# The skip term D u in a scan's gate: a TensorE product with a diagonal, or one VectorE operation on the sum in PSUM

## The chip, the cores and the metric

The kernel runs on one core of a Trainium2 chip (trn2). The metric is the device time of one execution in microseconds. Three executions of the kernel before took 5039.27, 5041.66 and 5051.98 us; the median, 5041.66 us, is the time before.

## The reference, cut to what matters

The input x holds 8 images of 384 channels by 32 x 32 pixels, so 1024 tokens each. Layer 0 is a Mamba block (a selective scan with 16 states per channel) that runs over the tokens forward and, with the same weights, backward; a depthwise convolution stands beside it. Layer 1 is causal attention with 6 heads and, on the first five images, a feed-forward part with binarized weights. All in fp32.

```python
u = silu((uc + conv1d_b[None, :, None]).transpose(0, 2, 1))
...
h = dA * h + dBu
return (h, jnp.einsum('bdn,bn->bd', h, c))
...
y = ys.transpose(1, 0, 2) + u * D_param
y = y * silu(z)
return jnp.einsum('bld,od->blo', y, out_proj_w)
...
fwd = mamba(x_flat, *mparams)
bwd = jnp.flip(mamba(jnp.flip(x_flat, axis=1), *mparams), axis=1)
g = (fwd + bwd) * scale_mod
```

The line that the change concerns is `ys + u * D_param`: a skip term with one weight D per channel. As both directions share z and the output projection, the kernel adds the two directions before the gate: (y_fwd + y_bwd + D (u_fwd + u_bwd)) silu(z).

## The kernel before, in words

Channels lie on the 128 partitions, in 3 chunks (c), tokens on the free axis in 2 halves of 512 (h). `before_scan` makes, for each image, the normed input, the projections, the two convolved u, their sum "us", the gate z and the scan's inputs, and leaves them in DRAM. `attention` and `feed_forward` are layer 1. The scan is cut into 768 units of two states each, one channel chunk, one direction and one half. A unit goes through six steps:

- `s_load` and `s_row` (L112) bring the inputs; SP issues all these loads in one queue.
- `s_first` (L588): POOL multiplies to g, 128 x 1024. There are six buffers for g.
- `s_scan`: ACT makes the decay da in PSUM (L601), DVE scans it, twice 512 elements (L606), POOL weighs g with C's rows (L612).
- `s_sum` (L620): PE transposes g in eight 128 x 128 blocks and adds them up in the one PSUM bank "y". At the end of a run ACT copies y into a tile yt (L635) or DVE adds it to one (L639).
- `s_gate` (L641 to L671), at the last unit of each channel chunk and half, so 48 times: it loads us and z (tags with one buffer each), takes a bank with the tag "pt" (two banks, shared with attention's transposes and others), puts the skip term and the transposes back of the two yt into it, multiplies the gate z by it on DVE (L668), and stores the product (L670).

In the kernel before, the skip term is a product on PE (L654): us is the moving operand, 128 x 512, and the stationary one is diagd, three 128 x 128 matrices with D on their diagonal, built once by DVE at the start (L183). It opens the bank's accumulation, and the eight transposes (L659, two yt of four blocks) add to it.

The order of the work is a merged list. `slots` puts the steps of neighbouring units together, `spread_over` and the list `timed` weave them between the steps of layer 1 by costs that are written with each step. The Tile framework then schedules each engine's instructions by its own model, so that an edit in one step can move others: the final order in the engines' queues isn't the order of the text. [...]`pin` keeps some instructions in the order of the program.

Of the kernel before, what the change touches and what calls it, by code (L numbers as in the profile page):

```python
# [12 lines left out]
ALU = mybir.AluOpType  # L13
# [4 lines left out]
P = 128  # L18
B, C, H, W = 8, 384, 32, 32
L = H * W  # L20
NC = C // P
# [28 lines left out]
V_NORM, V_CW, V_CB, V_DTB, V_D, V_DW, V_DWB, V_BP, V_B2, V_ALOG = 0, 1, 5, 6, 7, 8, 17, 18, 19, 20  # L50
# [4 lines left out]
def kernel(  # L55
# [16 lines left out]
    nc = tc.nc  # L72
# [11 lines left out]
    def ctile(name, shape, dt=F32):  # L84
        return const.tile(shape, dt, name=name, tag=name)
# [13 lines left out]
    def bank(name, tag=None):  # L99
        if tag is None:  # L100
            turn[0] += 1
            tag = ("s", "pt")[turn[0] % 2]
        return ps.tile([P, HB], F32, name=name, tag=tag, bufs=BANKS[tag])

    def half(h):
        return slice(h * HB, (h + 1) * HB)

    def chunk(c):
        return slice(c * P, (c + 1) * P)

    def load(dst, src):
        nc.sync.dma_start(out=dst, in_=src)  # L112
# [17 lines left out]
    vec = ctile("vec", [P, NC, NV])  # L130
# [8 lines left out]
    for d in range(2):  # L139
        nc.scalar.dma_start(out=wdt[d * DW : d * DW + RANK, :], in_=w_dt)  # L140
        nc.scalar.dma_start(
            out=wdt[d * DW + RANK : d * DW + RANK + 1, :],
# [13 lines left out]
    ident = ctile("ident", [P, P])  # L156
# [21 lines left out]
    amat = ctile("amat", [P, NC, NS])  # L178
    nc.scalar.activation(amat, vec[:, :, V_ALOG : V_ALOG + NS], AF.Exp)
    nc.vector.tensor_scalar(amat, amat, -1.0, None, ALU.mult)  # L180
    diagd = ctile("diagd", [P, NC, P])
    for c in range(NC):
        nc.vector.tensor_scalar(diagd[:, c, :], ident, vec[:, c, V_D : V_D + 1], None, ALU.mult)  # L183
    rssm = ctile("rssm", [P, 1])
    nc.vector.tensor_tensor(rssm, sc[:, 0:1], sc[:, 1:2], ALU.mult)
    rsh = ctile("rsh", [P, 1])
# [454 lines left out]
    def s_gate(u):  # L641

        if not u.last:
            return
        b, c, h = u.b, u.c, u.h
        yts = sst.pop(("yt", b, c, h))
        both = []
        for what in ("us", "z"):
            t = sp.tile([P, HB], F32, name=f"{what}h_{u.name}", tag=what, bufs=1)
            load(t, spilled[b, what, c][:, half(h)])  # L650
            both.append(t)
        us, sz = both
        tp = bank(f"yb_{u.name}", "pt")
        nc.tensor.matmul(  # L654
            out=tp, lhsT=diagd[:, c, :], rhs=us, start=True, stop=False, skip_group_check=True
        )
        for yt in yts:
            for i in range(QT):
                nc.tensor.matmul(  # L659
                    out=tp[:, chunk(i)],  # L660
                    lhsT=yt[:, i, :],
                    rhs=ident,
                    is_transpose=True,
                    start=False,
                    stop=(yt is yts[-1] and i == QT - 1),
                    skip_group_check=True,
                )
        nc.vector.tensor_tensor(sz, sz, tp, ALU.mult)  # L668
        t = dram.tile([P, HB], F32, name=f"sgy_{u.name}", tag=f"sp_gy_{c}_{h}")
        nc.sync.dma_start(out=t, in_=sz)  # L670
        spilled[b, "gy", c, h] = t  # L671
# [421 lines left out]
    def slots(lo, hi):  # L1093
        def at(f, k):
            if 0 <= k < len(units):
                f(units[k])

        def slot(k):
            at(s_load, k + AHEAD + 2)
            at(lambda u: s_row(u, 0), k + AHEAD + 2)  # L1100
            at(lambda u: s_row(u, 1), k + 2)
            at(s_first, k + AHEAD)
            at(s_scan, k)
            at(s_sum, k - 1)
            at(s_gate, k - 1)

        return [(lambda k=k: slot(k), 5.0) for k in range(lo, hi)]
# [113 lines left out]
```

## Time and profile before

The profiled execution took 5052.48 us, its span from the first to the last instruction is 5050.7 us. The mean granted TensorE clock is 0.883 of full speed.

| what | value |
|---|---|
| median of the runs | 5041.66 us |
| profiled execution / its span | 5052.48 / 5050.7 us |
| busy PE, DVE, ACT, POOL | 4072.5, 3605.3, 2667.4, 3689.9 us |
| L654, product with the diagonal | x96 records, 57.3 us busy, mean 683 ns |
| L659, transposes back in the gate | x384, 63.5 us busy, mean 303 ns |
| L668, gate product on DVE | x48, 32.0 us busy, mean 667 ns |
| L635, ACT's copy of y to yt | x96, 55.7 us busy, mean 580 ns |
| DMA | 696.35 MB, mean 138 GB/s |

How it is read: a group's line gives the file's line, the engine, what is written from what, the count, the busy time and the mean of one, and then the idle time of the engine just before these instructions with what ended it (the releaser). An fp32 matmul shows as two records, so 48 products are 96 records. Matmuls overlap in the records: what one holds of PE's queue is better read from its start to the next one's start. A line of waits reads "who waited <- for whom: us in total, times, longest".

### The profile page before, as it was taken

To read this page: it belongs to the slowest core of one execution; us is meant where nothing else is said; L and a number is where in the kernel's file an instruction comes from. 1 tells how busy PE (TensorE), PEld (TensorE's weight loads), DVE (VectorE), ACT (ScalarE), POOL (GpSimd) and SP (SyncE) were. 2 spreads that over 40 slices of the span, in tenths; PEclk is the share of its full clock that TensorE was granted. 3 is DMA by queue.
4 is the path that set the end of the run, shared out by engine and by line. 5 is a ranking of instruction groups with operands and counts; after the bars stand their busy time and mean duration, and the time that the engine had idled before them with its cause. 6 is when DMAs were issued, how large, how long until landed. Compare 5 with 4: busy or idle time off the path is not lost. (4 is left out here: it accounts for less than half of the span.)

```text
span 5050.7 us, 50731 instructions
## 1 busy us (share of the span) xinstructions
PE 4072.5 (81%) x16458; PEld 2180.7 (43%) x16458; DVE 3605.3 (71%) x4775; ACT 2667.4 (53%) x4850; POOL 3689.9 (73%) x1944
## 2 busy tenths in 40 slices
PE   4687787888888888788788888887787978978899
PEld 1243343444444444344444444443454444444444
DVE  6887988676887767786778867688766666676623
ACT  4565664564554655545656446555465355464426
POOL 0578687896868976778876688867788988888700
PEclk7788797989889889888999889998898989989999
DMA  6554546323453334463334633334533334334210
GB/s 227 204 175 160 200 155 229 109 88 118 152 187 135 119 115 154 139 200 111 103 134 143 213 111 128 110 123 155 194 132 106 118 108 143 109 101 139 88 58 26
DMA packets 365009, 696.35 MB, mean 138 GB/s; under 512 B 30104, under 2 KB 88904, under 8 KB 364744
## 3 DMA queue, kind: packets, MB, share of 16 engines
q1 hardware_dynamic: 355232, 676.97, 40.0%
q10 hardware_dynamic: 9512, 16.15, 0.9%
q8 instruction: 130, 2.13, 0.2%
q14 instruction: 135, 1.11, 0.1%
HBM read 527.33 MB, written 165.68 MB: 137 GB/s over the span
## 5 line engine op out<-in xcount | busy, mean ns | idle before, releaser
L588 POOL TENSOR_TENSOR g<-ud,bc 128x1024 f32<-128x1024 f32 x768 | 1837.9, 2393 | 654.0 <-PE y L620 523.0
L612 POOL TENSOR_TENSOR g<-g,bc 128x1024 f32<-128x1024 f32 x768 | 1819.4, 2369 | 194.9 <-DVE g L606 132.4
L601 ACT ACTIVATE da<-dl,amat 128x512 f32<-128x512 f32 x1536 | 1055.9, 691 | 1515.1 <-DVE g L606 1489.8
L606 DVE TENSOR_TENSOR_SCAN g<-da,g 128x512 f32<-128x512 f32 x768 | 907.7, 1210 | 509.6 <-POOL g L588 496.3
L606 DVE TENSOR_TENSOR_SCAN g<-da,carry,g 128x512 f32<-128x512 f32 x768 | 955.1, 1271 | 403.9 <-POOL g L588 374.5
L620 PE MATMUL y<-ident,g 128*128 128x128 f32 x6144 | 920.6, 297 | 210.3 <-POOL g L612 122.3
L620 PEld LDWEIGHTS y<-ident,g 128*128 128x128 f32 x6144 | 766.9, 153 | 644.3 <-issue 345.5
L786 PE MATMUL s<-k,q 64*128 64x512 f32 (+3 forms) x1152 | 394.6, 602 | 134.6 <-DVE nm L800 113.5
L800 DVE CUSTOM_DVE_ANT_0 pr<-s,cmask 128x512 f32<-128x512 f32 (+3 forms) x576 | 298.9, 544 | 179.3 <-PE s L786 159.9
L810 ACT ACTIVATE pr<-pr,nm 128x512 f32<-128x512 f32 (+3 forms) x576 | 348.4, 606 | 125.1 <-DVE nm L800 123.5
L862 PE MATMUL pt<-ident,pr 128*128 128x128 f32 x1728 | 302.1, 304 | 83.5 <-ACT ptn L864 38.5
L992 PE MATMUL hp<-t,w 128*128 128x512 f32 x720 | 339.3, 618 | 25.4 <-DMA w<-w1s 21.2
L1036 PE MATMUL yp<-h,w 128*128 128x512 f32 x720 | 331.9, 620 | 32.0 <-DMA w<-w2s 27.6
L341 PE MATMUL in<-xn,win 128*128 128x512 f32 x576 | 291.2, 651 | 36.5 <-DVE xc L463 15.9
L862 PEld LDWEIGHTS pt<-ident,pr 128*128 128x128 f32 x1728 | 207.0, 152 | 243.5 <-ACT ptn L864 94.3
L875 PE MATMUL av<-ptn,v 128*64 128x512 f32 (+3 forms) x1152 | 274.3, 559 | 23.2 <-DVE o L889 17.2
L611 POOL COPY carry<-g 128x2 f32<-128x2 f32 x384 | 87.7, 228 | 271.2 <-DVE g L606 271.2
L864 ACT COPY ptn<-pt 128x512 f32<-128x512 f32 (+3 forms) x576 | 254.7, 473 | 55.5 <-PE pt L862 53.5
L725 PE MATMUL qp<-t,wqk 128*128 128x512 f32 x576 | 267.8, 616 | 14.7 <-DVE t L302 12.5
L400 DVE SCALAR_TENSOR_TENSOR loc<-xn,vec,loc 128x496 f32<-128x496 f32 (+3 forms) x384 | 259.5, 722 | 20.3 <-ACT loc L389 19.0
L786 PEld LDWEIGHTS s<-k,q 64*128 64x128 f32 x1152 | 134.8, 206 | 266.5 <-DVE nm L800 190.1
L1036 PEld LDWEIGHTS yp<-h,w 128*128 128x128 f32 x720 | 141.9, 201 | 204.7 <-issue 177.2
(153 smaller groups left out, 4753.4 us busy)
## 6 DMA issues: line engine op xcount, KB each, us to landing
bc<-rows SPq DMA_DIRECT2D x512, 512.0 KB, 4.1
dl<-sdl SPq DMA_DIRECT2D x160, 256.0 KB, 2.9
ud<-sud SPq DMA_DIRECT2D x160, 256.0 KB, 2.7
t<-st SPq DMA_DIRECT2D x63, 512.0 KB, 5.1
su<-u SPq DMA_DIRECT2D x48, 512.0 KB, 3.6
du<-su SPq DMA_DIRECT2D x96, 256.0 KB, 3.8
sdl<-du SPq DMA_DIRECT2D x96, 256.0 KB, 2.9
sud<-du SPq DMA_DIRECT2D x96, 256.0 KB, 2.7
```

The lines of the kernel that those rows point to most:

```text
L341: nc.tensor.matmul(out=mp, lhsT=st["win", c][:, k, i, :], rhs=st["xn"][:, k, half(h)], start=(k == 0), stop=(k == NC - 1),)
L588: pin(nc.gpsimd.tensor_tensor(g, ud, sst["bc", 0, u.b, u.part, u.n], ALU.mult))
L601: nc.scalar.activation(da, sst["dl", u.b, u.c, u.part], AF.Exp, scale=amat[:, u.c, n : n + 1])
L606: nc.vector.tensor_tensor_scan(gi[:, ::step], da[:, ::step], gi[:, ::step], first, ALU.mult, ALU.add)
L612: pin(nc.gpsimd.tensor_tensor(g, g, sst["bc", 1, u.b, u.part, u.n], ALU.mult))
L620: nc.tensor.matmul(out=y[:, j, :], lhsT=g[:, i, chunk(j)], rhs=ident, is_transpose=True, start=(u.opens and i == 0 and j == 0), stop=(u.cl ...
L786: mm = nc.tensor.matmul(out=ss[e][:, : k1 - k0], lhsT=st["q"][rows_of(e), c, chunk(qi)], rhs=st["k"][rows_of(e), c, k0:k1], start=True, st ...
L800: nc.vector.tensor_tensor_reduce(out=x, in0=ss[e][:, :w], in1=mask, scale=-1.0, scalar=-MASKED, op0=ALU.add, op1=ALU.min, accum_out=m,)
L810: nc.scalar.activation(x, x, AF.Exp, bias=m, scale=-1.0, accum_out=rs[:, i, e, kb : kb + 1])
L862: nc.tensor.transpose(pt[:, chunk(i)], pr[:, e, chunk(j % QT)], ident)
L992: nc.tensor.matmul(out=hp, lhsT=st["w1"][:, c, chunk(m % 2)], rhs=st["xn"][:, c, half(h)], start=(c == 0), stop=(c == NC - 1),)
L1036: nc.tensor.matmul(out=yp, lhsT=st["w2", k // 6][:, k % 6, :], rhs=st["h", k // NC][:, k % NC, half(h)], start=(k == 0), stop=(k == NF - 1),)
```

## The change

The diagonal matrices and the products with them are taken out. The first transpose of the gate now opens the bank's accumulation. Behind the transposes one DVE operation (scalar_tensor_tensor) computes us times D, D being a column with one value per partition, plus the sum in PSUM, and writes it back to the same bank; the gate product follows as before.

```diff
-    diagd = ctile("diagd", [P, NC, P])
-    for c in range(NC):
-        nc.vector.tensor_scalar(diagd[:, c, :], ident, vec[:, c, V_D : V_D + 1], None, ALU.mult)
...
         us, sz = both
         tp = bank(f"yb_{u.name}", "pt")
-        nc.tensor.matmul(
-            out=tp, lhsT=diagd[:, c, :], rhs=us, start=True, stop=False, skip_group_check=True
-        )
         for yt in yts:
             for i in range(QT):
                 nc.tensor.matmul(
...
                     is_transpose=True,
-                    start=False,
+                    start=(yt is yts[0] and i == 0),
                     stop=(yt is yts[-1] and i == QT - 1),
                     skip_group_check=True,
                 )
+        nc.vector.scalar_tensor_tensor(tp, us, vec[:, c, V_D : V_D + 1], tp, ALU.mult, ALU.add)
         nc.vector.tensor_tensor(sz, sz, tp, ALU.mult)
```

## The prediction

> **What bounds the kernel now.** I read the page's head first, then the table of who waits for whom on POOL and DVE, then every gate (the end of a scan, where the skip term enters) in the timeline, then the stretches around the gates.
>
> ```profile
> PE 4072.5 (81%) x16458; PEld 2180.7 (43%) x16458; DVE 3605.3 (71%) x4775; ACT 2667.4 (53%) x4850; POOL 3689.9 (73%) x1944
> ```
>
> No engine is full. PE is the busiest, and the scan runs in a ring: POOL makes g (L588), DVE scans it (L606), POOL weighs it (L612), PE adds it into y (L620), and that frees the buffer for POOL. Who is late in the ring is read from POOL's waits:
>
> ```profile
> POOL g L588 <- PE y L620: 523.0, 203, 16.0
> POOL carry L611 <- DVE g L606: 271.2, 28, 49.0
> POOL g L612 <- DVE g L606: 132.4, 18, 26.8
> ...
> POOL g L588 <- DVE g L606: 7.5, 4, 6.9
> ```
>
> POOL waits 523.0 us for PE and 271.2 + 132.4 + 7.5 = 411 us for DVE. So PE is the later partner in 523 / 934 = 0.56 of it, DVE in 0.44. These are my shares for how much of a change on either engine reaches the end. DVE in turn waits 870.8 us for POOL's L588: it often has time over.
>
> Now one gate of image 1, in the timeline of all engines (start, length, engine, line, operation, in brackets the idle time before it and its releaser):
>
> ```profile
> 1763.00 1.09 PE L620 MATMUL y<-ident,g 128*128 128x128 f32 x8
> ...
> 1763.93 1.02 PE L654 MATMUL yb<-ush,diagd 128*128 128x512 f32 x2
> ...
> 1764.79 0.60 PE L659 MATMUL yb<-ident,yt 128*128 128x128 f32 x4
> ...
> 1767.23 0.56 ACT L635 COPY yt<-y 128x512 f32<-128x512 f32 x1
> ...
> 1767.84 1.05 PE L659 MATMUL yb<-ident,yt 128*128 128x128 f32 x4 [2.45 <-ACT yt L635]
> 1767.91 2.34 DVE L606 TENSOR_TENSOR_SCAN g<-da,g 128x512 f32<-128x512 f32 x2 [1.61 <-POOL g L588]
> ...
> 1770.16 0.66 DVE L668 TENSOR_TENSOR zh<-zh,yb 128x512 f32<-128x512 f32 x1
> ...
> 1771.72 0.42 PEld L862 LDWEIGHTS pt<-ident,pr 128*128 128x128 f32 x4 [0.90 <-DVE zh L668]
> ```
>
> The diagonal product comes right behind the last y and holds PE's queue for 1764.79 - 1763.93 = 0.86 us. Then PE turns the first partial sum (four transposes) and stands for the second one, which ACT copies only at 1767.23. In 22 of the 48 gates PE stands there, 58.7 us in all. DVE's gate product comes late, behind two scans, and PE's next pt bank waits for it.
>
> **What the Trainium skill says.** "VectorE: DVE Perf Modes", section "Why PSUM operands drop a tier": an fp32 operation with an operand in PSUM runs at the plain rate of one element per cycle. Its errata section gives (N+151)/0.96 ns for an fp32 tensor_tensor, 691 ns at 512. The trace agrees roughly: L668 took 667 ns, and the form that the change adds is there as L369 (tile in SBUF, scalar column, sum read and written in PSUM): 746 ns. The same page, "The DRAIN you can't avoid", says that the next DVE operation doesn't start before the pipe is empty. Here it starts a little earlier: 0.58 to 0.60 us behind the start of L668, and seven L369 in a row took 4.70 us, 0.67 each. The measurement decides: 0.66 us of queue. "TensorE: Matmul & The Clock Gate", section "Architectural detail: the array is 16× 32×32, not 1× 128×128": PE pulls only weight loads forward, and DVE and ACT are strict FIFO. The gate above agrees: PE stood 2.45 us with other matmuls ready behind.
>
> **The change part by part.** *Removed on PE:* 48 products, recorded as 96 matmuls of 683 ns mean (57.3 us busy, overlapping). From each product's start to the next instruction's, they hold the queue 49.5 us: 0.86 each at full clock, 48 x 0.86 = 41.3, and 8.2 more in gates at half clock. What that saves depends on whether PE stands for yt behind it. I keep the times at which yt was ready. In the changed order of instructions, 39 gates have other PE work between the first and the second four transposes (7 before), so the place of the product is taken by work that had to be done anyway:
> - 21 gates without a stall (yt was early, or other work now covers its copy): 21 x 0.86 = 18.1 us.
> - 18 gates with a stall or long filler: product out, filler in, stall about as before: from 0.34 to 1.5 us each, 13.5 us.
> - 3 gates in part: in two there is no filler and the product was what covered ACT's copy, in one fillers stood there already: 1.0 us.
> - 6 gates nothing: PE waits there for the same yt, for POOL or for h.
> Sum 32.6 us of PE queue. With the share 0.56 that is 18.3 us at the end; with all of it passed on, 32.6, or 40.8 with the half-clock part.
>
> *Added on DVE:* 48 scalar_tensor_tensor of 0.66 us queue, 31.7 us (35.8 by full duration). In the 5 us from the gate product's start DVE is idle for 0.75 us or more in 32 gates: hidden, in idle time that is mostly the wait for POOL. If that cover is gone they cost their 21 us. The other 16 gates, ten of them before 1405 us, have none: 16 x 0.66 = 10.6, times 0.44 = 4.7 us. In 16 gates the new operation stands one or two scans earlier in DVE's order than the product did, so scans queue behind its wait for PE's transposes, and ACT's exponentials behind the scans. L668 waited for yb only 6 times, 21.8 us; I put no more on this and leave it to the slower rival.
>
> *The pt bank is held longer.* PE waited for L668 in 12 places, 15.7 us. Each may grow by 0.66, 7.9 us; the changed order puts y transposes ahead of several of these waits, so I take half, times 0.56: 2.2 us.
>
> *Moved on SP.* The us buffer is single and now comes free after the new DVE operation instead of after the product, so the next load of us waits some us longer (6.2 us from product to L668 in the gate above). SP waited 131.5 us for L654, and 182.0 us for L668 in the store next to it. Behind stand row loads and scan loads; POOL waited for a row load once, 2.4 us. Nothing, unless SP falls behind by more than the loads are early.
>
> *Start and tail.* Three diagonal builds of 282 ns fall away at 15 us, where DVE waits for its first data (11.7 us for the scales): nothing, or 0.8 us without that wait. At the last gate (4828.8) the end hangs on DVE: L668 at 4834.21, a store, a load of gy, then op at 4841.18. The new operation and one yq product now lie ahead of it: 0.66 + 0.70 = 1.4 us, in full.
>
> *Sum:* -18.3 + 4.7 + 2.2 + 1.4 = -10.0 us. The profiled execution took 5052.5 (span 5050.7), so 5042.5. It lies 10.8 us, 0.2%, above the median; the same difference on 5041.66 gives 5031.7, which I round to 5032. Measurement can tell about 0.3%, 15 us, from no change.
>
> **The rivals.** *PE decides throughout.* For it: POOL waits 203 times for PE, PE's matmuls only 57 times for L612. Against: in stalled gates yt itself waits in ACT's queue behind exponentials that wait for DVE. Then the full 40.8 us, less the tail: -39.4, so 5002. *DVE decides (slower).* The place is the gate in DVE's FIFO: the new operation waits for transposes that now come behind filler, with scans, ACT's exponentials and yt behind it. For it: between 740 and 830 us DVE is busy 82.7 of 90 us, and 16 gates have scans behind the new operation. Against: DVE's 870.8 us of waits for POOL. Price: 31.7 on DVE, 7.9 at pt, 1.4 tail, with only the 21 clean gates kept (18.1 x 0.56 = 10.1): +31, so 5073. With my PE gain, no change is reached when (18.3 - 3.6) / 31.7 = 0.46 of DVE's added time is on the path; I put 0.15 there. *The order alone.* Beside the 48 products, 342 matmuls and more than 200 instructions each of DVE and ACT stand elsewhere in their queues. No row prices this; I allow 15 us either way, and it can hide everything above.
>
> **Chances.** Forecast 0.52, with its own range 5017 to 5047 (of it 0.18 faster than 5026.5, 0.33 within, 0.01 slower than 5056.8); PE throughout 0.22; DVE decides 0.21 (0.19 slower, 0.02 within); order alone 0.05 (0.02 faster, 0.03 slower). Faster 0.42, same 0.35, slower 0.23. The range leaves about a tenth on each side: from close to the PE case, 5004, to between no change and the DVE case, 5064.
>
> **What would show it.** Right: no L654; PE busy lower by about 57; stalls for yt about as before, near 59; POOL's waits for y shorter by some 18; a DVE row with about 0.74 us x48 whose wait for PE stays near 22. Wrong: POOL's waits for DVE or DVE's wait for yb up by 20 or more (DVE case), or POOL's wait for y down by over 35 with nothing new (PE case). If waits move by tens of us in stretches without gates, the order decided.

## The result, and the profile after

The changed kernel takes 4999.8 us in the median (4987.9 to 5003.1, four runs); the kernel before, run beside it, 5040.5 us (5037.1 to 5052.0, four runs). The ratio is 0.9911 [0.9888, 0.9934]: about 41 us or 0.9% faster. The interval leaves no doubt of the sign. The time lies 4 us below the low end of the predicted range, and close to the rival "PE decides throughout" (5002), not to the forecast (5032).

The profiled execution of the changed kernel took 5002.11 us (span 5000.3, clock 0.881). That of the kernel before (5052.48) lay some 12 us above its median and that of the changed kernel 2, so the two spans differ by 50.4 us, and some 10 of them belong to these two executions.

The page's head after:

```profile
PE 4035.3 (81%) x16362; PEld 2172.5 (43%) x16362; DVE 3640.4 (73%) x4820; ACT 2666.1 (53%) x4850; POOL 3693.8 (74%) x1944
```

PE is busy for 37.2 us less (4072.5 before) and has 96 records less; DVE is busy for 35.1 us more. The span fell by 50.4: 37.2 of it is PE's work, and 13.2 is idle time of PE that went as well. Now POOL's waits for its partners in the ring (L588 of before is L585 now, L611 is L608, L612 is L609, L606 is L603, L620 is L617):

```profile
POOL g L585 <- PE y L617: 471.6, 174, 18.5
POOL carry L608 <- DVE g L603: 264.5, 28, 50.0
...
POOL g L609 <- DVE g L603: 119.3, 18, 24.8
...
POOL g L585 <- DVE g L603: 7.3, 3, 6.9
```

The wait for PE fell from 523.0 to 471.6, by 51.4 us; that for DVE from 411 to 391. DVE has more to do, and yet POOL waits for it no longer than before. What was won stands for the most part in the one row.

The same gate of image 1 as was shown of before, now in the changed kernel's timeline (start, length, engine, line, operation, idle time before it and its releaser):

```profile
1766.24 1.09 PE L617 MATMUL y<-ident,g 128*128 128x128 f32 x8
...
1767.17 0.60 PE L653 MATMUL yb<-ident,yt 128*128 128x128 f32 x4
...
1767.70 0.87 PE L842 MATMUL f<-ident,rs 128*64 128x128 f32 x10
...
1770.46 0.56 ACT L632 COPY yt<-y 128x512 f32<-128x512 f32 x1
...
1771.08 1.06 PE L653 MATMUL yb<-ident,yt 128*128 128x128 f32 x4 [2.51 <-ACT yt L632]
...
1773.39 0.73 DVE L662 SCALAR_TENSOR_TENSOR yb<-ush,vec,yb 128x512 f32<-128x512 f32 x1
...
1774.16 0.69 DVE L663 TENSOR_TENSOR zh<-zh,yb 128x512 f32<-128x512 f32 x1
```

The product is gone from between the last y and the first four transposes. Behind these four, ten matmuls of attention (L842) now stand, which stood behind the gate before, and then PE waits 2.51 us for ACT's copy of the second yt: product out, other work (the filler) in, stall as before (2.45). DVE's new operation comes with the gate product right behind it, 0.77 us later. What this gate gains is the filler that is done early; its stall is as long as before.

Over all gates the stall for yt (PE's idle time before the transposes of a gate, until ACT has copied the partial sum) did not stay, though. PE's, DVE's and SP's waits at the gate in the changed kernel:

```profile
PE yb L653 <- ACT yt L632: 35.3, 16, 8.5
...
DVE yb L662 <- PE yb L653: 20.2, 3, 8.8
```

```profile
SPq L112 <- DVE yb L662: 245.7, 33, 46.6
```

PE's stall for yt was 58.7 us in 22 gates and is 35.3 in 16. DVE's wait for the transposes is about as it was (21.8). SP waits 245.7 us for the us buffer instead of 131.5, but 44.6 instead of 182.0 for the gate product next to it: together 290.3 instead of 313.5. POOL's waits for row loads went from 2.4 us once to 12.7 in three places.

**Where in the span the time goes.** POOL runs its 768 first steps (L588, now L585) in the same order in every kernel here, so the start of the n-th one (counted from 0) is a ruler. The table has the start in the kernel without the product less the start in its partner with it, in us. The second and third pair come from experiments 8 to 11 below: one cost number of the merged list is 10.6 or 10.8 there and not 10.7, in both kernels of the pair.

| POOL step, start before (us) | after - before | same pair, order 10.6 | same pair, order 10.8 |
|---|---|---|---|
| 90, 735 | -2.6 | -1.6 | -4.1 |
| 103, 831 | +6.0 | +6.5 | +5.9 |
| 144, 1052 | +5.0 | +4.7 | +6.3 |
| 192, 1355 | +3.2 | +4.4 | +5.5 |
| 201, 1421 | -0.5 | +1.2 | +4.7 |
| 264, 1784 | +1.3 | +2.6 | +1.2 |
| 312, 2111 | -10.5 | -5.2 | -10.6 |
| 384, 2528 | -15.1 | -18.8 | -15.3 |
| 480, 3119 | -25.4 | -27.0 | -25.0 |
| 576, 3728 | -38.5 | -32.8 | -37.2 |
| 672, 4249 | -43.1 | -36.8 | -42.3 |
| 767, 4802 | -50.4 | -43.7 | -40.3 |

The first 12 gates, up to 1405 us, gave nothing in sum, but not evenly. From 735 to 831 us, where gates 4 to 6 lie, the kernels without the product fall back by 8 to 10 us. POOL's waits for loads from 735 to 860 us, in the kernel before and then in the changed one:

```profile
POOL g L612 <- DMA bc<-rows: 2.4, 1, 2.4
```

```profile
POOL g L609 <- DMA bc<-rows: 8.4, 2, 7.9
...
POOL g L585 <- DMA ud<-sud: 6.7, 1, 6.7
POOL g L585 <- DMA bc<-rows: 4.3, 1, 4.3
```

That is 19.4 us in place of 2.4; in the other two pairs it is 17.9 and 18.4 in place of 2.5. The us buffer is not among SP's waits from 720 to 840 us in the changed kernel. The longest of them there is for DVE's du (21.6 us, 23.2 before), which SP stores in the same queue; why the loads come later stays open. Gates 7 to 12 then give 6.5, 5.3 and 1.2 us back.

All of the gain comes after 1760 us. The products of the 36 later gates held 35.9 of the 49.5 us of PE's queue. In the six stretches with these gates (1760:1980, 2370:2570, 2970:3160, 3580:3770, 4090:4290, 4620:4800) the ruler falls by 43.6, 38.7 and 35.8 us in the three pairs, so they paid in full or more, and between these stretches by another 10.0, 10.6 and 7.7.

Most of the reason stands in POOL's waits of the kernel before, cut by stretches. Up to 830 us (partner DVE in the first two lines, PE in the last):

```profile
POOL carry L611 <- DVE g L606: 123.5, 13, 49.0
...
POOL g L612 <- DVE g L606: 39.1, 7, 18.8
POOL g L588 <- PE y L620: 24.0, 9, 5.7
```

From 2370 to 2570 us, where six gates lie, the only wait listed:

```profile
POOL g L588 <- PE y L620: 35.6, 18, 6.4
```

And from 4090 to 4290 us, again:

```profile
POOL g L588 <- PE y L620: 34.8, 17, 6.5
```

In the early stretch, with the first six gates, POOL waits for DVE 162.6 us and for PE 24.0, a share of PE of 0.13. From 830 to 1420 us, with gates 7 to 12, it waits for PE 76.3 us and for DVE 39.0, a share of 0.66. In the six later stretches it waits for PE 40.2 + 35.6 + 26.1 + 20.6 + 34.8 + 32.3 = 189.6 us and for DVE 36.8: a share of 189.6 / 226.4 = 0.84, not 0.56. Cut at the same POOL steps in the changed kernel, the 189.6 us are 150.6. So 39.0 of the 51.4 us by which POOL's wait for PE fell lie in these six stretches, and 4.4 between 830 and 1420.

### The profile page after: what moved, and what is told of

Its sections match the earlier page's. It is cut to its first block, busy times and chain, and to the rows that moved or that the text cites. A ratio compares the mean times of both kernels' runs of the same rounds, so it can differ in the third digit from the quotient of the medians.

```text
span 5000.3 us, 50609 instructions
## 1 busy us (share of the span) xinstructions
PE 4035.3 (81%) x16362; PEld 2172.5 (43%) x16362; DVE 3640.4 (73%) x4820; ACT 2666.1 (53%) x4850; POOL 3693.8 (74%) x1944
## 5 line engine op out<-in xcount | busy, mean ns | idle before, releaser
L585 POOL TENSOR_TENSOR g<-ud,bc 128x1024 f32<-128x1024 f32 x768 | 1840.9, 2397 | 613.6 <-PE y L617 471.6
L609 POOL TENSOR_TENSOR g<-g,bc 128x1024 f32<-128x1024 f32 x768 | 1821.4, 2372 | 187.7 <-DVE g L603 119.3
L603 DVE TENSOR_TENSOR_SCAN g<-da,g 128x512 f32<-128x512 f32 x768 | 908.3, 1211 | 498.1 <-POOL g L585 481.8
L603 DVE TENSOR_TENSOR_SCAN g<-da,carry,g 128x512 f32<-128x512 f32 x768 | 956.1, 1271 | 368.1 <-POOL g L585 339.9
L617 PE MATMUL y<-ident,g 128*128 128x128 f32 x6144 | 932.5, 299 | 220.3 <-POOL g L609 133.8
L617 PEld LDWEIGHTS y<-ident,g 128*128 128x128 f32 x6144 | 774.8, 154 | 653.8 <-issue 344.3
L987 PE MATMUL hp<-t,w 128*128 128x512 f32 x720 | 343.3, 622 | 26.7 <-DMA w<-w1s 20.2
L1031 PE MATMUL yp<-h,w 128*128 128x512 f32 x720 | 331.8, 620 | 27.4 <-DMA w<-w2s 27.4
L608 POOL COPY carry<-g 128x2 f32<-128x2 f32 x384 | 85.8, 223 | 264.6 <-DVE g L603 264.5
L397 DVE SCALAR_TENSOR_TENSOR loc<-xn,vec,loc 128x496 f32<-128x496 f32 (+3 forms) x384 | 259.3, 722 | 19.6 <-ACT loc L386 18.4
```

The costliest lines, as they stand in the source:

```text
L585: pin(nc.gpsimd.tensor_tensor(g, ud, sst["bc", 0, u.b, u.part, u.n], ALU.mult))
L603: nc.vector.tensor_tensor_scan(gi[:, ::step], da[:, ::step], gi[:, ::step], first, ALU.mult, ALU.add)
L609: pin(nc.gpsimd.tensor_tensor(g, g, sst["bc", 1, u.b, u.part, u.n], ALU.mult))
L617: nc.tensor.matmul(out=y[:, j, :], lhsT=g[:, i, chunk(j)], rhs=ident, is_transpose=True, start=(u.opens and i == 0 and j == 0), stop=(u.cl ...
L987: nc.tensor.matmul(out=hp, lhsT=st["w1"][:, c, chunk(m % 2)], rhs=st["xn"][:, c, half(h)], start=(c == 0), stop=(c == NC - 1),)
L1031: nc.tensor.matmul(out=yp, lhsT=st["w2", k // 6][:, k % 6, :], rhs=st["h", k // NC][:, k % NC, half(h)], start=(k == 0), stop=(k == NF - 1),)
```

## The experiments

The theory after the result (A in the expectations): PE decides at the later gates, and the queue time taken from it comes out nearly whole; DVE's operation is free there. Its rivals: both parts count and partly cancel (B); or the change of order gave the time, with the product having little to do with it (C). Ratios are to the kernel before on the same chip.

**1. No skip term at all (e1_no_skip).** The changed kernel without its new DVE operation; D u is left out, and us is still loaded.

```diff
-        nc.vector.scalar_tensor_tensor(tp, us, vec[:, c, V_D : V_D + 1], tp, ALU.mult, ALU.add)
```

> The skip term D u is left out altogether: no product, no DVE operation (us is still loaded), so the output lacks D u. Theory A (PE's queue time comes out in full, the DVE operation is hidden): as the changed kernel, 4990 to 5005. Theory B (half of PE's time comes out, DVE's 32 us cost a part): the DVE operation away should give 10 to 15 us more, 4980 to 4990. Theory C (the order of the queues decides): anything, and waits change in stretches without gates.

Measured: 5004.07 us, ratio 0.9928 [0.9913, 0.9943], DVE busy 3602.0. Without the operation the kernel is no faster than with it. So the 31.7 us that it holds of DVE's queue cost nothing that this run could show. It isn't the operation alone, though: by the traces, PE's order differs from the changed kernel's in 290 of 16362 records (those outside the longest common order), and run 8 shows what order can do.

**2. The DVE operation beside the product (e2_both).** The kernel before, with the operation added ahead of the gate product, at a factor of 0.

```diff
+        nc.vector.scalar_tensor_tensor(tp, us, 0.0, tp, ALU.mult, ALU.add)
         nc.vector.tensor_tensor(sz, sz, tp, ALU.mult)
```

> The kernel before, with its product, and the DVE operation beside it with factor 0 (so it adds nothing): the DVE operation alone. Theory A: hidden, within 10 us of 5040. Theory B (my forecast's share): 5 to 14 us slower, 5045 to 5054. If DVE decided: 5065 to 5075.

Measured: 5047.98, ratio 1.0012 [1.0004, 1.0021], so +2 to +11 us. In the order of before the operation costs a little at most: PE's waits for the gate product, which frees the pt bank, were 15.7 us in the kernel before; here they are 21.7 at the transposes of pt and 4.6 at xp.

**3. The product twice (e3_twice).** The kernel before, with half D on the diagonal and the product made twice.

```diff
-        nc.vector.tensor_scalar(diagd[:, c, :], ident, vec[:, c, V_D : V_D + 1], None, ALU.mult)
+        nc.vector.tensor_scalar(diagd[:, c, :], ident, vec[:, c, V_D : V_D + 1], 0.5, ALU.mult, ALU.mult)
...
-        nc.tensor.matmul(
-            out=tp, lhsT=diagd[:, c, :], rhs=us, start=True, stop=False, skip_group_check=True
-        )
+        for n in range(2):
+            nc.tensor.matmul(
+                out=tp,
+                lhsT=diagd[:, c, :],
+                rhs=us,
+                start=(n == 0),
+                stop=False,
+                skip_group_check=True,
+            )
```

> The product twice, each with D/2, no DVE operation: 48 more products on PE, about 41 us of its queue at full clock and 50 with the half-clock gates. Theory A (PE's queue time one to one): 5080 to 5090. Forecast's share 0.56: 5063 to 5068. Theory C' (a product ahead of a stall for yt costs nothing because the stall shrinks by it): 5040 to 5055.

Measured: 5069.97, ratio 1.0059 [1.0044, 1.0075], +27 us by the medians of this set (5042.65 before) and +30 by the ratio. The page's head and the stall for yt in this kernel:

```profile
PE 4101.6 (81%) x16554; PEld 2196.1 (43%) x16554; DVE 3606.6 (71%) x4775; ACT 2667.2 (53%) x4849; POOL 3686.7 (73%) x1944
```

```profile
PE yb L665 <- ACT yt L635: 36.0, 19, 6.5
```

A second product costs less than its own queue time, and part of it runs while PE would have stood: the stall fell from 58.7 to 36.0 us. Its 41.3 to 49.5 us of queue less 22.7 is 19 to 27, near the measured 27 to 30.

**4. The later partial sum turned first (e5_last_first).** The changed kernel with the two yt in the other order.

```diff
-        for yt in yts:
+        for yt in reversed(yts):
...
-                    start=(yt is yts[0] and i == 0),
-                    stop=(yt is yts[-1] and i == QT - 1),
+                    start=(yt is yts[-1] and i == 0),
+                    stop=(yt is yts[0] and i == QT - 1),
```

> The changed kernel with the two partial sums turned in the other order, the last one first, so that PE has nothing of the gate to do before the late copy; in its queue no other work lies between the two sets of four transposes (39 gates in the changed kernel, none here). If the product's absence alone gives the gain (A): 4995 to 5010. If it is the work that the new order put into the stall for yt (C): the gain is mostly gone, 5025 to 5045.

Measured: 5009.36, ratio 0.9935 [0.9918, 0.9952], stall for yt 37.8 us. The edit was to take the filler away and didn't: in the trace, other PE work stands between the two fours in no gate (in 39 in the changed kernel), but ahead of all eight in 39 (in 5 there). So work between the fours isn't needed for the gain; whether work ahead of the late transposes is needed, this run doesn't tell.

**5. The changed kernel again (after_again).**

> The changed kernel once more, as the measure for the runs beside it: 4990 to 5008 by every theory.

Measured: 4998.83, ratio 0.9908 [0.9892, 0.9924]. The gain holds in a second set of runs, with a narrower interval.

**6. One sum in place of two tiles (e7_one_sum).** In the changed kernel, DVE adds the last run's y to the first run's tile, where ACT copied it to a tile of its own; PE turns one tile per gate, not two.

```diff
-        if u.run == 0 or u.last:
-            tag = {"tag": "yl", "bufs": 1} if u.last else {"tag": "yt", "bufs": 2 * NC}
-            yt = sp.tile([P, QT, P], F32, name=f"yt_{u.name}", **tag)
+        if u.run == 0:
+            yt = sp.tile([P, QT, P], F32, name=f"yt_{u.name}", tag="yt", bufs=2 * NC)
```

> The changed kernel, and DVE adds the last partial sum to the first (as it does for the middle ones) in place of ACT's copy, so that PE turns one tile back and not two: 192 of 384 transposes fewer, 4 x 0.11 = 0.44 us of PE's queue in each of 48 gates, 21 us; DVE has 48 x 0.67 = 32 us more, ACT 28 us less. Theory A (PE's queue time comes out one to one, DVE is hidden): 20 us below the changed kernel, near 4980. With 0.6 to 0.7 of it: 4985 to 4988. If the wait for the partial sum is what counts, it stays, now for DVE: 4995 to 5010.

Measured: 4988.55, ratio 0.9892 [0.9875, 0.9909]; PE busy 4005.8. PE's wait at the transposes in this kernel, now for DVE's sum:

```profile
PE yb L652 <- DVE yt L635: 59.8, 23, 12.2
```

PE is busy for 29.5 us less than in the changed kernel, the stall at the transposes is 24.5 us longer, and the median falls by about 10 us; the intervals overlap. Most of the PE work that was removed here doesn't show at the end. The edit also moves the last sum from ACT to DVE, so it isn't a clean test of PE's queue alone.

**7. The copy of yt ahead in ACT's queue (e8_copy_first).**

```diff
-            nc.scalar.copy(yt, y)
+            with tc.high_priority(offset=HURRY) if u.last else nullcontext():
+                nc.scalar.copy(yt, y)
```

> The changed kernel with ACT's copy of the last partial sum at high priority, so that it stands ahead of the exponentials in ACT's queue; all work as before. If PE's stall for the copy (35 us in the changed kernel) is on the path: 10 to 25 us less, 4975 to 4990. If PE's queue time alone counts (A): as the changed kernel within 8.

Measured: 4992.74, ratio 0.9895 [0.9879, 0.9911]. The stall for yt is 33.4 us, against 35.3: the edit didn't do what it was for, so this doesn't tell what the stall is worth.

**8. Another order alone (e9_order).** The kernel before, with another number at one cost in the feed-forward part; the same instructions, of which about 180 of PE's 12364 stand elsewhere in its queue.

```diff
-                @emit.of(10.7)
+                @emit.of(10.6)
```

> The kernel before with one planner cost of the feed-forward part at 10.6 in place of 10.7: the same work, but about 180 of 12364 matmuls stand elsewhere in PE's queue. What a change of order alone does. Theory A and B: within 10 us of 5042. Theory C: 15 us or more, either way.

Measured: 5023.34, ratio 0.9962 [0.9948, 0.9976]: 19 us less with no work removed. The order alone is worth half of what the change gave, so a single pair couldn't settle the theory against this rival. Hence more pairs.

**9 to 12. The change in other orders.** f1_after_106 is the changed kernel with 10.6 in that place. f2_before_108 and f3_after_108 are both kernels with 10.8. f4_twice_106 is the doubled product of run 3 with 10.6.

> The changed kernel with the planner cost at 10.6, the partner of the kernel before at 10.6 (5023 where the kernel before took 5042). If the product's going is worth the same in each order (35 to 45 us): 4978 to 4990. If the gain was the luck of one order: 5000 to 5025.

> The kernel before with the planner cost at 10.8: a third order of the same work (147 matmuls elsewhere). A change of order alone: somewhere in 5020 to 5050.

> The changed kernel with the planner cost at 10.8, the partner of the run before it. If the product's going is worth the same in each order: 35 to 45 us below its partner. If order decides: within 20 us of it.

> The product twice, each with D/2, with the planner cost at 10.6. If PE's queue time counts at 0.7 to 1: 30 to 45 us above its partner's 5023, so 5053 to 5068. If order decides: within 20 us of it.

| order | product | none (DVE operation) | difference | product twice | difference |
|---|---|---|---|---|---|
| 10.7 | 5040.5 | 4999.8 | -40.7 | 5069.97 | +27.3 |
| 10.6 | 5023.34 | 4981.65 | -41.7 | 5049.59 | +26.3 |
| 10.8 | 5062.59 | 5013.32 | -49.3 | not run | |

(Ratios: f1 0.9883 [0.9869, 0.9898], f2 1.0047 [1.0033, 1.0061], f3 0.995 [0.9935, 0.9965], f4 1.0022 [1.0013, 1.0031]. The 10.6 row sets runs of different chips side by side, and the +27.3 is taken from the kernel before of its own set, 5042.65; by the ratios to the kernel before, these three differences are -40, +30 and +30.) Taking the product out gives 40 to 49 us in three orders, while the orders themselves differ by 32 to 39 us. Doubling costs 26 to 30 in two, with the stall for yt going from 60.1 to 38.9 us at 10.6 as it went from 58.7 to 36.0 at 10.7. The number 10.6 takes 17 to 20 us from all three kernels and 10.8 adds 22 and 14, so the order adds to or takes from both sides roughly alike.

No run takes the product out and leaves PE's order as it was. By the longest common order of PE's records in the traces, without the product's, the change itself moves 395 of 16362. But the kernels without the product of runs 1, 4 and 13 differ from the changed kernel in 290, 435 and 403 records, and all four lie at ratios of 0.9907 to 0.9935. The gain goes with the product's absence and hangs on no single order; that the scheduler finds better places once the product is gone may be a part of it.

**13. Four DVE operations at each gate (g1_dve_four).** The changed kernel with three more, at a factor of 0.

```diff
         nc.vector.scalar_tensor_tensor(tp, us, vec[:, c, V_D : V_D + 1], tp, ALU.mult, ALU.add)
+        for _ in range(3):
+            nc.vector.scalar_tensor_tensor(tp, us, 0.0, tp, ALU.mult, ALU.add)
```

> The changed kernel with three more DVE operations of the same form behind the one (factor 0, so they add nothing): 48 x 3 x 0.66 = 95 us more on DVE. If DVE's time in the gate is hidden: within 15 us of the changed kernel's 4999. If it counts at 0.15 (my forecast's part): 5013. At 0.44: 5041. If all: 5094.

Measured: 4998.62, ratio 0.9907 [0.9893, 0.992]: the changed kernel's time. Its page's head, its operations on the bank and its waits in the ring:

```profile
PE 4047.5 (81%) x16362; PEld 2165.9 (43%) x16362; DVE 3737.5 (75%) x4964; ACT 2667.4 (53%) x4848; POOL 3693.0 (74%) x1944
```

```profile
L664 DVE SCALAR_TENSOR_TENSOR yb<-ush,yb x144: 665/686/697, 588.7 to 4780.2; 128x512 f32<-128x512 f32 x144
L662 DVE SCALAR_TENSOR_TENSOR yb<-ush,vec,yb x48: 725/744/756, 587.5 to 4776.5; 128x512 f32<-128x512 f32 x48
```

```profile
DVE g L603 <- POOL g L585: 720.5, 417, 11.9
...
POOL g L585 <- PE y L617: 415.9, 156, 14.2
...
POOL carry L608 <- DVE g L603: 286.9, 36, 48.7
```

DVE is busy for 97.1 us longer, and the 97 us come out of its wait for POOL: 821.8 to 720.5. POOL waits 22.4 us longer for DVE at its carry, but 55.7 us less for PE: so what it loses to one partner it mostly would have waited for the other. This is the clearest of the runs on DVE: three more operations like the change's own at every gate, at no time that can be measured. DVE's time in full would have made it 5094. The forecast's share of 0.15, 5013, lies within what an order can do (run 8), and is spoken against by runs 1 and 13 together, not by one alone.

**14. The filler tied behind the gate (g2_nofill).** The changed kernel; the next 20 matmuls or transposes that the program issues after a gate are kept behind it.

```diff
+BEHIND = 20
...
+    after_gate = [0]
+    class Te:
+        def matmul(self, **k):
+            ins = nc.tensor.matmul(**k)
+            if after_gate[0] > 0:
+                after_gate[0] -= 1
+                pin(ins)
+            return ins
...
         nc.vector.scalar_tensor_tensor(tp, us, vec[:, c, V_D : V_D + 1], tp, ALU.mult, ALU.add)
+        after_gate[0] = BEHIND
```

> The changed kernel with the next 20 matmuls of the program behind each gate tied behind it in PE's queue, so that in 32 gates nothing stands between the last y and the transposes that need the copy (4 gates in the changed kernel, 36 before). If the work put into PE's stall is a good part of the gain: 5015 to 5030. If the product's queue time alone: 4995 to 5010. The ties move other matmuls too, so a difference under 20 us says little.

Measured: 5090.0, ratio 1.0096 [1.0083, 1.011], 91 us above the changed kernel. Its stall for yt:

```profile
PE yb L79 <- ACT yt L651: 81.5, 36, 8.9
```

With the filler held back, PE stands in 36 gates in place of 16. But the stall grew by 46 us and the time by 91: the ties move 622 of PE's 16362 records against the changed kernel (by the longest common order of the two traces), and the stalls alone don't account for the time. So the freedom to reorder is worth a lot here, and how much of it lies in the filler at the gates stays open.

**15. Both improvements (g3_one_sum_106).** Run 6 with 10.6.

> One tile turned back and not two (DVE adds the last partial sum), with the planner cost at 10.6: both gains together. If they add up: 4965 to 4975; if order swamps it: 4980 to 5000.

Measured: 4983.46 (4961.5 to 4989.6), ratio 0.9873 [0.9854, 0.9891]. It has the lowest ratio of all runs, 1.3% under the kernel before, but isn't told apart from f1_after_106 (0.9883): one sum and the other order don't clearly add up.

## Why the prediction was wrong

The sign was right and the size was not: -10.0 us was forecast and -40.7 measured. The prediction had 40.8 us for the case that all of PE's queue time is passed on. From this the forecast took 30.8 us off, in the three places below. That 40.8 lies so near the measured time is in part luck. It leaves out 8.7 of the 49.5 us, at gates that were taken to give nothing or less than the product's time, and it doesn't know of the 8 to 10 us that are lost from 735 to 831 us.

- **The share 0.56 (14.3 us of it: 32.6 - 18.3). This step failed.** It was taken from POOL's waits over the whole span, where 411 us are for DVE. But 162.6 of these lie before 830 us, in few long waits of up to 49 us. In the stretches of the later gates the share is 0.84. The ruler shows both sides: the first six gates, where DVE is late, gave nothing, and the stretches of the later 36 gave 36 to 44 us for 35.9 us of queue. The prediction itself had read that ten of the gates without cover on DVE lie before 1405 us, and yet used one mean for all. With 0.84 on the same 32.6 us the term had been 27.4. Taken stage by stage on the queue time in the trace, an estimate is 0.13 x 7.9 + 0.66 x 5.7 + 0.84 x 35.9 = 35 us.
- **The half-clock part (8.2 us: 40.8 - 32.6).** The prediction named it and then left it out of its sum without a reason. The trace of before has both cases: a product holds PE's queue for 1.71 us at 2996 us, where the granted clock was 0.50, and for 0.86 us at 3018 us, where it was 1.00. Of the 8.2 us, 4.9 lie in the 36 later gates. No run measures this part by itself.
- **The charges on DVE +4.7 and on the pt bank +2.2, and the tail +1.4 (8.3 us).** Run 2 found +2 to +11 in the order of before, so the size wasn't foolish there. In the order after, runs 1 and 13 found none for the first two: leaving the operation out wins nothing, and four of them cost nothing. PE's wait for the gate product, expected to grow, fell from 15.7 us in 12 places to 6.4 in 5; in the gate shown, y transposes now stand ahead of it. From POOL's last step to the end the three pairs differ by 0.0, +3.4 and +1.5 us, so the tail's 1.4 is not refuted.

Within the 32.6 us one reading failed as well, in the other direction. The prediction saw that 39 gates would get other work between the two fours (7 before), and counted it, but took the stalls for yt to stay, near 59 us. Single gates do that: in the gate shown, 2.45 us became 2.51. In the sum they don't: 58.7 us became 35.3, and PE's idle time fell by 13 us with its work. Runs 3 and 12 show that added work can hide in this stall, 21 to 23 us of it. That the filler shortened the stall fits these numbers, but was only argued: neither run 4 nor run 14 isolated it.

What held: PE's 96 records went; DVE's row came at 732 ns in the median (0.74 expected), its wait for PE at 20.2 us (near 22 expected). PE's busy time fell by 37.2 us, not 57: in the trace of before, the time in which PE is busy with nothing but the product is 41.7 us, as its records overlap others'. The term for SP, put at nothing unless its loads fell behind, is where they did fall behind: POOL's 19.4 us of waits for loads come with 8.6 us lost on the ruler, though not shown to come from the us buffer. The prediction had named a wait for y down by over 35 with nothing new as the mark of the PE case, and that is nearly what came: -51.4, of which some 10 belong to the two profiled executions, with the waits for loads as the one thing new.

**The rivals.** "PE decides throughout" gave the right time with a reason that holds for the later 36 gates, in two of the three pairs from gate 7 on, and not for the first six. "DVE decides" is refuted by run 13. "The order alone" was thought to be worth 15 us either way, at a chance of 0.05; one number moved the kernel before by -19 and another by +22. It didn't make this result by itself, as three pairs show, but with that spread it should have widened the range on both sides.

**Open.** What the filler and the freer order are worth by themselves; why 8 to 11 us more came between the stretches with later gates; why the loads come later from 735 to 860 us; and whether the first gates would pay if DVE had less to do there, which wasn't tried.

## What to carry to other kernels

Read who is late in the stretches where the change lies: a share of waits over the span mixes stages with other limits, and here it was 0.56 where the late gates had 0.84 and the first six 0.13. Adding and removing need not be mirror images once a scheduler may reorder: the same product cost 26 to 30 us to add, part of it hidden in a stall, and its exchange for the DVE operation gave 40 to 49. The gap is small against the intervals, and plain removal (run 1) gave 36 to 39. Where the order of instructions is found by a model, move one of its numbers and test the pair in two or three orders before crediting an edit with less than some 20 us.

## What the runs showed of the hardware

The same DVE operation on 128 x 512 fp32 with its sum in PSUM takes 744 ns in the median with a column as its scalar and 686 ns with a constant (the two rows of run 13, same execution). And an engine that is busy for 73% of the span, on a ring with two other engines, took 97 us more work without an effect on the end that could be measured (run 13).
